# A selective scan on one core: units of 32 channels by 4 states in place of 8 channels by 16 states

## The chip, the core and the metric

The kernel runs on one core of a Trainium2 chip. A core has five engines that work from queues of their own, each in its own order: TensorE (PE), VectorE (DVE), ScalarE (ACT), GpSimd (POOL) and SyncE (SP), which here issues all the DMAs. The DMAs are carried by 16 DMA engines that the queue shares out. The metric is device time in microseconds (us) of one launch; lower is better.

## The reference, cut to what matters

The input is a batch of 8 images of 64 x 64 tokens with 192 channels. Two layers follow each other. Layer 0 is a state-space layer whose scan the kernel computes by matrix products over chunks, followed by a small MLP. Layer 1 splits the channels: one half goes through three convolutions, the other half through a depthwise convolution and a selective scan in four directions, a layer norm, a gate and a projection. The change touches only the selective scan of layer 1:

```python
D_HALF, D_INNER, D_STATE, DT_RANK, K = (96, 192, 16, 6, 4)
x_dbl = jnp.einsum('bkdl,kcd->bkcl', xs4, x_proj_w)
dts = x_dbl[:, :, :DT_RANK]
Bs = x_dbl[:, :, DT_RANK:DT_RANK + D_STATE]
Cs = x_dbl[:, :, DT_RANK + D_STATE:]
delta = jax.nn.softplus(jnp.einsum('bkrl,kdr->bkdl', dts, dt_proj_w) + dt_proj_b[None, :, :, None])
A = -jnp.exp(A_logs)

def step(h, t):
    u_t, d_t, b_t, c_t = t
    h = jnp.exp(d_t[..., None] * A) * h + (d_t * u_t)[..., None] * b_t[:, :, None, :]
    return (h, jnp.einsum('bkdn,bkn->bkd', h, c_t))
...
ys = jnp.moveaxis(ys, 0, -1) + Ds[None, :, :, None] * xs4
```

Each of 8 images has 4 directions, 192 channels and 16 states, so 8 x 4 x 192 x 16 = 98,304 sequences of 4,096 tokens. Each needs a decay exp(delta A), an input delta u B, the recurrence, a product with C and a sum over the 16 states. delta and u depend on the channel, B and C on the state; a unit of 128 partitions that holds channels and states together must have all four repeated to the shape of the unit.

## The kernel before

A unit of the scan is one tile of 128 partitions by 1,024 tokens (`LC`). Its partitions are 8 channels (`UD`) by 16 states: partition 8n + c is state n of channel c. There are 3,072 units: 8 images, 2 pairs of directions, 4 pieces of 1,024 tokens, 3 tiles of 128 channels (`t` = 0, 2, 1; two directions of a pair share the three tiles) and 16 units in each tile. `steps` are the pairs and pieces, `tiles` the tiles, and `units` numbers all units with q.

For each tile, `prepare` makes delta (softplus on ACT, L1406) and du = delta u on POOL (L1409), stores delta to DRAM (`dld`, L1412), splits du into three bf16 terms (two casts on ACT, L1417 and L1421, two subtractions on POOL, L1419 and L1423), stores those (`dud`, L1426) and loads them back in 12 DMAs as `dus` (L1434). For each step, `project` computes the rows of B, C and dt by matmul and stores B and C to DRAM (`bcd`), and `lay` (L1386) loads each back repeated to 128 partitions.

For each unit q the work is:

- `fetch` (L1445): one DMA of 512 KB brings 8 rows of delta, repeated 16 times, from DRAM into a `dA` tile. It is issued six units ahead (`AHEAD`), into seven buffers.
- `decay` (L1450): ACT turns that tile in place into exp(delta A), two units ahead.
- `spread` (L1458): PE spreads du over the states into PSUM `dB`, two matmuls, one unit ahead, in two buffers.
- `weigh` (L1473): DVE multiplies `dB` in PSUM with the repeated B.
- `scan` (L1480): DVE runs the recurrence; then POOL multiplies h with C in place, on all columns but the last (L1482).
- `carry_on` (L1488, L1489): ACT copies the last column to the carry of the next piece and then multiplies that column with C.
- `gather` (L1500): every four units PE sums over the states, in two halves of four matmuls side by side in 32-column groups; ACT copies each half out of PSUM (L1505), and four DMAs of 8 rows store it (`store`, L1513).

Layer 0 of the next image and the rest of layer 1 of other images run beside the scan. `Beside` holds them as generators; after each half unit `half` lets them issue instructions until a credit in estimated PE time is used up, so every engine's queue interleaves scan and side work in the order in which the Python code issues them (`pin` keeps that order). All DMAs stand in SP's queue in the same order. PSUM has eight banks: four rotate among all side work and the scan's small results (`cx.one`), four are the two buffers of `dB`.

The repeating DMAs have their source pattern from `repeated`:

```python
n = rows.shape[0]
row, col = [list(d) for d in rows.ap]
dims = [row, [0, 128 // n]] if inner else [[0, 128 // n], row]
return bass.AP(rows.tensor, rows.offset, dims + [col])
```

The outermost dimension of the source is thus the number of copies in `fetch` and the number of rows in `lay`; the destination is 128 partitions of 4 KB.

Of the kernel before, what the change touches and what calls it, by code (L numbers as in the profile page):

```python
# [39 lines left out]
UD = 128 // NS  # L40
UN = 128 // UD
# [68 lines left out]
def setup(cx, cp, dp, p0, p1):  # L110
# [141 lines left out]
    fold = cp.tile([128, UD], F32, tag="fold", name="fold")  # L252
    nc.vector.tensor_copy(fold, ident[:, 0:UD])
    for i in [32 * g + UD * v for g in range(4) for v in range(3)][1:]:
        nc.vector.tensor_add(fold, fold, ident[:, i : i + UD])
    for g in range(4):
        nc.vector.tensor_copy(
            k["spread"][32 * g : 32 * (g + 1), :].rearrange("p (n c) -> p n c", c=UD),
            bcast(fold[32 * g : 32 * (g + 1), 0:UD], 1, NS),
        )  # L260
    col = cp.tile([128, UD], F32, tag="col", name="col")
    nc.vector.tensor_copy(col, ident[:, 0:UD])
    for n in range(1, NS):
        nc.vector.tensor_add(col, col, ident[:, UD * n : UD * (n + 1)])
    k["gather"] = cp.tile([128, 32], F32, tag="gather", name="gather")
    nc.gpsimd.memset(k["gather"], 0.0)
    nc.vector.tensor_copy(k["gather"][:, 0:UD], col)
# [110 lines left out]
def conv0(cx, x):  # L378
# [3 lines left out]
    with cx.pool("cw0") as wp, cx.pool("v0", 2) as vp:  # L382
# [51 lines left out]
        def convolve(p, j):  # L434
            pss = [cx.one("ps_cv") for i in range(2)]
            yield from depthwise(cx, pss, [diag[0:64, j], diag[64:128, j]], pads[j])
            for i, ps in enumerate(pss):
                xc = xcs[p, 2 * j + i] = vp.tile([128, 512], F32, tag="xc", name="xc", bufs=7)
                pin(nc.scalar.activation(xc, ps, AF.Silu, bias=k["cb"][:, 2 * j + i : 2 * j + i + 1]))
# [73 lines left out]
def ssd(cx):  # L513
# [16 lines left out]
    with cx.pool("g0", 2) as gp, cx.pool("s0", 2) as sp:  # L530
# [126 lines left out]
        def outputs(c):  # L657
# [19 lines left out]
            yield None  # L677
            psh = [cx.one("ps_h")[:, :INNER0] for d in range(2)]
# [7 lines left out]
            ps = pss[1].rearrange("p (h c) -> p h c", c=HP)  # L686
            pin(nc.vector.tensor_add(Hn, ps, Hn))
# [31 lines left out]
def mlp0(cx, x, x1):  # L719
# [9 lines left out]
    with cx.pool("mw0") as wp, cx.pool("m0", 2) as mp:  # L729
# [8 lines left out]
        def loads(i):  # L738
# [10 lines left out]
            def load_y(v, d):  # L749
                t = mp.tile([128, 2, INNER0], F32, tag=f"y{d}", name=f"y{d}", bufs=4 - 2 * d)  # L750
# [561 lines left out]
def selective_scan(cx, us, ys, beside, images, start_image, tail):  # L1312
# [9 lines left out]
    AHEAD, BEHIND = 6, 2  # L1322
# [6 lines left out]

    units = [(n, i) for n in range(len(tiles)) for i in range(UN)]  # L1330
    U = len(units)
# [12 lines left out]
    with (  # L1344
# [4 lines left out]
        tc.tile_pool(name="ps1w", bufs=2, space=PSUM) as pw,  # L1349
    ):  # L1350
        u_of, rows_of, bc_of, delta_of, du_of, carries = {}, {}, {}, {}, {}, {}
        dAs, dBs, hs, late = {}, {}, {}, []
# [7 lines left out]
        def project(m):  # L1360
# [15 lines left out]
            yield  # L1376
            yield
            bcd = dp.tile([4 * NS, LC], F32, tag="bcd", name="bcd")
            pin(nc.sync.dma_start(out=bcd, in_=rows[0 : 4 * NS]))
            rows_of[m] = rows, bcd  # L1380

        def lay(m, e, i):

            t = wp.tile([128, LC], F32, tag=f"bc{i}{e}", name=f"bc{i}{e}")
            at = NS * (2 * i + e)
            pin(nc.sync.dma_start(out=t, in_=repeated(rows_of[m][1][at : at + NS], True)))  # L1386
            bc_of.setdefault((m, e), []).append(t)

        def prepare(n):
# [8 lines left out]
            dl, du = (wp.tile([128, LC], F32, tag=v, name=v) for v in ("dl", "du"))  # L1398
            pss = [cx.one("ps_dt") for here in halves]
            for ps, at, here in zip(pss, DTS, halves):  # L1400
                took = slice(at, at + 2 * RK)
                pin(nc.tensor.matmul(ps, lhsT=k["dtw"][took, g, t, :], rhs=rows[took, here], start=True, stop=True))
            beside.spend(1.2)
            yield 1
            for ps, here in zip(pss, halves):
                pin(nc.scalar.activation(dl[:, here], ps, AF.Softplus, bias=bias))  # L1406
            cx.exp_again()
            yield 3
            pin(nc.gpsimd.tensor_mul(du, dl, u_of[m][t]))  # L1409
            yield 6  # L1410
            dld = dp.tile([128, LC], F32, tag="dld", name="dld")
            pin(nc.sync.dma_start(out=dld, in_=dl))  # L1412
            delta_of[n] = dld
            yield 7

            terms = wp.tile([128, 3, LC], BF16, tag="terms", name="terms")
            pin(nc.scalar.copy(terms[:, 0, :], du))  # L1417
            yield 9
            pin(nc.gpsimd.tensor_sub(du, du, terms[:, 0, :]))  # L1419
            yield 11  # L1420
            pin(nc.scalar.copy(terms[:, 1, :], du))  # L1421
            yield 13
            pin(nc.gpsimd.tensor_sub(terms[:, 2, :], du, terms[:, 1, :]))  # L1423
            yield 17
            dud = dp.tile([3, 128, LC], BF16, tag="dud", name="dud")
            pin(nc.sync.dma_start(out=dud.rearrange("s p l -> p s l"), in_=terms))  # L1426
            yield 21

            dus = np_.tile([128, UN // 2, 512], BF16, tag="dus", name="dus")
            for half in range(2):  # L1430
                for odd in range(2):
                    at = 32 * (2 * odd + half)
                    for v in range(3):
                        pin(nc.sync.dma_start(  # L1434
                            out=dus[at + UD * v : at + UD * (v + 1)],
                            in_=dud[v].rearrange("(i odd c) l -> odd c i l", odd=2, c=UD)[odd][:, :, halves[half]],
                        ))
# [82 lines left out]
        for i in range(2):  # L1520
            lay(0, 0, i)
# [217 lines left out]
```

## Time and profile before

| what | value |
|---|---|
| median of 3 runs | 16,427.84 us (16,426.35 to 16,461.0) |
| profiled execution, first to last instruction | 16,436.7 us |
| PE busy | 13,372.1 us, 81% of the span |
| DVE busy | 12,230.0 us, 74% |
| POOL busy | 10,527.5 us, 64% |
| ACT busy | 10,412.7 us, 63% |
| DMA, main queue | 3,227.83 MB in 1,601,496 packets, 78.5% of 16 engines' span |
| mean granted TensorE clock | 0.827 of full speed |
| scan, 3,072 times on DVE (L1480) | 2,344 ns each, 7,200.8 us |
| product with B on DVE (L1473) | 1,216 ns each, 3,736.3 us |
| product with C on POOL (L1482) | 2,354 ns each, 7,228.8 us |
| decay on ACT (L1450) | 1,144 ns each, 3,512.9 us |
| sum over the states on PE (L1500) | 730 ns each, 4 side by side, 2,364.1 us |

The profile lists the span of the profiled execution and no other time of it; the span is 0.05% above the median of the runs. The busy times are unions over the span: a PE that is busy may be waiting in its pipeline. The first scan starts at 902 us and the last at 16,193 us, so the span has about 870 us in front of the scan stage and 240 us behind it. Between them a unit takes 5.0 us on average, of which DVE has 3.56 us for the two operations of the scan. In the tables of idle time, the engine or DMA named after an arrow is the one whose end released the waiting instruction.

### The profile page before, as it was taken

The page shows a single profiled execution, that of the slowest core. Times are in us where ns is not written, and L with a number is a line of the kernel's source. Part 1 is how long each engine was busy: PE and PEld are TensorE (multiplying, and loading weights), DVE is VectorE, ACT ScalarE, POOL GpSimd, SP SyncE. Part 2 cuts the span into 40 slices and gives each one's busy share as a digit, 9 for nine tenths or more (in the row PEclk, how much of TensorE's full clock was granted, in tenths as well). Part 3 has the DMA queues.
Part 4 walks back from the last instruction along what each step waited for, and adds up shares of the span by engine and source line. Part 5 has one row for each costly group of instructions (what it writes and reads, how often), then busy time and mean ns, then how long its engine had stood idle before and what let it go on. Part 6 is the DMA issues. An engine that isn't in the chain of part 4 may idle for free.

```text
span 16436.7 us, 210821 instructions
## 1 busy us (share of the span) xinstructions
PE 13372.1 (81%) x69608; PEld 4636.5 (28%) x69608; DVE 12230.0 (74%) x9264; ACT 10412.7 (63%) x20023; POOL 10527.5 (64%) x5766
## 2 busy tenths in 40 slices
PE   8977887788877897878888788777898788878876
PEld 4423322332223321333223332233322333211111
DVE  2178887886878767887678876788767886778994
ACT  4466677665775757757576575766657666655654
POOL 3158766775668656686567765677656775566773
PEclk9987888789887897878888798887988779877766
DMA  3288888788887888878888778887778877888885
GB/s 89 84 218 195 210 205 225 190 204 208 204 219 187 205 205 207 209 191 204 208 208 207 198 196 198 217 205 197 204 193 221 198 202 205 193 227 200 211 204 137
DMA packets 1602582, 3241.31 MB, mean 197 GB/s; under 512 B 390152, under 2 KB 841368, under 8 KB 1601496
## 3 DMA queue, kind: packets, MB, share of 16 engines
q1 hardware_dynamic: 1601496, 3227.83, 78.5%
q8 instruction: 559, 9.16, 0.3%
q14 instruction: 527, 4.32, 0.1%
HBM read 2548.91 MB, written 678.18 MB: 196 GB/s over the span
## 4 chain that ended last, share of the span: by engine, by line
PE 30%; DMA 16%; DVE 14%; ACT 13%; POOL 7%; issue 5%; SPq 2%; DVEq 0%; ACTq 0%; POOLq 0%
DVE h L1480 9%; DMA dA<-dld 5%; PE acc L1500 5%; DVE dB L1473 4%; PE ps_c L895 4%; PE ps_cv L343 3%; POOL h L1482 3%; ACT dA L1450 3%; PE dB L1458 2%; DMA dus<-dud 2%; PE ps_sum L1193 1%; ACT L107 1%; PE ps_m L799 1%; PE ps_y L696 1%; ACT h L830 1%
## 5 line engine op out<-in xcount | busy, mean ns | idle before, releaser
L1482 POOL TENSOR_TENSOR h<-h,bc 128x1023 f32<-128x1023 f32 x3072 | 7228.8, 2354 | 4585.2 <-DVE h L1480 3895.8
L1480 DVE TENSOR_TENSOR_SCAN h<-dA,carry,dB 128x1024 f32<-128x1024 f32 x3072 | 7200.8, 2344 | 820.7 <-ACT dA L1450 257.6
L1473 DVE TENSOR_TENSOR dB<-dB,bc 128x1024 f32<-128x1024 f32 x3072 | 3736.3, 1216 | 1827.5 <-PE dB L1458 1823.9
L1450 ACT ACTIVATE dA<-dA,neg_a 128x1024 f32<-128x1024 f32 x3072 | 3512.9, 1144 | 29.3 <-DMA dA<-dld 24.1
L1500 PE MATMUL acc<-h,gather 128*32 128x512 f32 x12288 | 2364.1, 730 | 596.5 <-ACT h L1489 329.0
L1458 PE MATMUL dB<-dus,spread 24*128 24x512 bf16 x6144 | 1370.2, 435 | 664.5 <-DVE h L1480 620.1
L1505 ACT COPY y<-acc 128x512 f32<-128x512 f32 x1536 | 884.8, 576 | 750.3 <-PE acc L1500 677.4
L895 PE MATMUL ps_c<-p,conv_w 96*96 96x512 f32 x2304 | 1287.7, 685 | 37.9 <-ACT p L915 26.9
L1488 ACT COPY carry<-h 128x1 f32<-128x1 f32 x3072 | 584.2, 190 | 856.9 <-DVE h L1480 854.4
L1458 PEld LDWEIGHTS <-spread 24*128 24x128 bf16 x6144 | 308.0, 93 | 2837.2 <-issue 1395.5
L1489 ACT ACTIVATE h<-h,bc 128x1 f32<-128x1 f32 x3072 | 905.2, 295 | 143.3 <-ACT carry L1488 1.8
L696 PE MATMUL ps_y<-X,M 64*64 64x64 f32 x12288 | 605.6, 270 | 418.6 <-issue 232.7
L624 ACT ACTIVATE M<-ps_d,ln_dt 128x64 f32<-128x64 f32 x3072 | 669.1, 335 | 314.6 <-PE ps_d L630 304.6
L343 PE MATMUL ps_cv<-pad,diag 64*64 64x512 f32 x6912 | 841.0, 605 | 7.1 <-ACT y L1505 5.1
L1500 PEld LDWEIGHTS acc<-h,gather 128*32 128x32 f32 x12288 | 311.2, 117 | 1636.3 <-issue 1040.1
L107 ACT ACT_TABLE_LOAD x577 | 740.3, 1283 | 10.0
L696 PEld LDWEIGHTS ps_y<-X,M 64*64 64x64 f32 x12288 | 548.8, 180 | 606.5 <-issue 275.5
L629 PE MATMUL ps_d<-R,after 128*128 128x384 f32 x1024 | 606.4, 685 | 31.2 <-ACT bc L618 14.6
L895 PEld LDWEIGHTS ps_c<-p,conv_w 96*96 96x96 f32 x2304 | 372.6, 180 | 785.5 <-issue 725.4
L618 ACT COPY bc<-ps_t 64x256 f32<-64x256 f32 x256 | 93.4, 365 | 716.7 <-PE ps_t L613 716.5
L373 PE MATMUL ps_h<-oa,w1a 128*128 128x256 f32 x1536 | 484.0, 438 | 76.6 <-ACT y L1505 32.2
L1370 PE MATMUL ps_xp<-u,xp 128*108 128x512 f32 x768 | 470.0, 699 | 92.5 <-DMA u<-u 76.0
(243 smaller groups left out, 18412.4 us busy)
## 6 DMA issues: line engine op xcount, KB each, us to landing
dA<-dld SPq DMA_DIRECT2D x3072, 512.0 KB
dud<-terms SPq DMA_DIRECT2D x192, 768.0 KB
dus<-dud SPq DMA_DIRECT2D x2304, 64.0 KB
bc<-bcd SPq DMA_DIRECT2D x256, 512.0 KB
y<-yrows SPq DMA_DIRECT2D x256, 384.0 KB
u<-u SPq DMA_DIRECT2D x192, 512.0 KB
dld<-dl SPq DMA_DIRECT2D x192, 512.0 KB
y<-y SPq DMA_DIRECT2D x3072, 32.0 KB
```

The lines of the kernel that those rows point to most:

```text
L107: self.pin(self.nc.scalar.preload_act_table_set("natural_log_exp_and_others"))
L343: pin(nc.tensor.matmul(ps[64 * b : 64 * (b + 1)].rearrange("p (h w) -> p h w", w=WW), lhsT=diag[:, t, :], rhs=pad[64 * i : 64 * (i + 1), b ...
L696: pin(nc.tensor.matmul(psy[d][here, h * HP : (h + 1) * HP], lhsT=M[here, d, h, :], rhs=X[here, d, h, :], start=True, stop=True,))
L895: pin(nc.tensor.matmul(ps.rearrange("p (h w) -> p h w", w=WW), lhsT=w[:, t, :], rhs=pad[:, dy : dy + RB, dx : dx + WW], start=t == 0, stop ...
L1450: pin(nc.scalar.activation(dAs[q], dAs[q], AF.Exp, scale=k["neg_a"][:, steps[m][1], t, i : i + 1]))
L1458: pin(nc.tensor.matmul(dBs[q][:, half, :], lhsT=k["spread"][at : at + 3 * UD, :], rhs=du_of[n][at : at + 3 * UD, i // 2, :], start=True, s ...
L1473: pin(nc.vector.tensor_mul(dBs[q], dBs[q], of(q)[0]))
L1480: pin(nc.vector.tensor_tensor_scan(order(h, g), order(dA, g), order(dB, g), carry, ALU.mult, ALU.add))
L1482: pin(nc.gpsimd.tensor_mul(h[:, rest], h[:, rest], C_[:, rest]))
L1489: pin(nc.scalar.activation(end, end, AF.Identity, scale=C_[:, last : last + 1]))
L1500: pin(nc.tensor.matmul(ps[32 * v : 32 * (v + 1)], lhsT=k["gather"], rhs=hs[q - 3 + v][:, here], start=True, stop=True))
L1505: pin(nc.scalar.copy(y[:, here], ps))
```

## The change

A unit becomes 32 channels by 4 states (partition 32n + c). A tile of 128 channels still has 16 units: 4 groups of channels, each with 4 units of 4 states. The order in a tile is by pairs of groups: 8 units (`GROUP`) take the four states of two groups in turn.

- delta and du are both fetched repeated: one DMA of 512 KB each for a group of 32 channels, used by its four units, in three buffers each (`dlr`, `dur`). The fetches for the next 8 units are issued at the odd units of the present 8: delta and du of the first group at units 1 and 3, of the second at units 5 and 7.
- B takes the place that du had: it is split into three bf16 terms on 32 rows in `project`, stored, loaded by `lay_b` in four small DMAs, and spread over the channels by `spread`. The terms of du and their casts, subtractions and DMAs are gone; du is made in place of u.
- C is laid by `lay_c`: four DMAs of 512 KB for each direction in place of one (4 rows, each repeated 32 times).
- The product with C goes to a new tile `g` (four buffers) and covers all columns; the second ACT operation of `carry_on` is gone, its copy is left out for the last piece, and it runs two units behind instead of one.
- `gather` runs every two units and adds the four states up in one PSUM tile of its own; one copy and two DMAs of 64 rows store a pair of groups.
- The rotating PSUM buffers go from four to three, `xc` from 7 to 6 buffers, `y0` and `y1` of the MLP from 4 and 2 to 3 and 2, `h` from 7 to 3, and one addition in `ssd` moves in front of two matmuls.

```diff
-UD = 128 // NS
-UN = 128 // UD
+UD = 32
+NU = 128 // UD
+UN = 128 // UD * (NS // NU)
...
-    AHEAD, BEHIND = 6, 2
+    BEHIND, GROUP = 2, 8
...
+        def of(q):
+
+            n, i = divmod(q, UN)
+            pair, i = divmod(i, GROUP)
+            state, b = divmod(i, 2)
+            return n, *tiles[n], 2 * pair + b, state
...
+        def lay_c(m, e, state):
+
+            t = wp.tile([128, LC], F32, tag=f"c{e}{state}", name=f"c{e}{state}")
+            at = NS * e + NU * state
+            pin(nc.sync.dma_start(out=t, in_=repeated(rows_of[m][2][at : at + NU], True)))
...
-        def fetch(q):
-            n, i = units[q]
-            dAs[q] = np_.tile([128, LC], F32, tag="dA", name="dA", bufs=AHEAD + 1)
-            pin(nc.sync.dma_start(out=dAs[q], in_=repeated(delta_of[n][UD * i : UD * (i + 1)], False)))
+        def fetch(q, which):
+
+            n, _, _, cg, _ = of(q)
+            tag = ("dl", "du")[which]
+            t = np_.tile([128, LC], F32, tag=tag + "r", name=tag + "r", bufs=3)
+            pin(nc.sync.dma_start(out=t, in_=repeated(delta_of[n][which][UD * cg : UD * (cg + 1)], False)))
+            reps[n, cg, which] = t
...
-            pin(nc.vector.tensor_mul(dBs[q], dBs[q], of(q)[0]))
+            pin(nc.vector.tensor_mul(dBs[q], dBs[q], reps[n, cg, 1]))
...
-            h = hs[q] = np_.tile([128, LC], F32, tag="h", name="h", bufs=4 + BEHIND + 1)
+            h = hs[q] = np_.tile([128, LC], F32, tag="h", name="h", bufs=3)
             pin(nc.vector.tensor_tensor_scan(order(h, g), order(dA, g), order(dB, g), carry, ALU.mult, ALU.add))
-            rest = slice(1, LC) if last == 0 else slice(0, LC - 1)
-            pin(nc.gpsimd.tensor_mul(h[:, rest], h[:, rest], C_[:, rest]))
+            gs[q] = np_.tile([128, LC], F32, tag="g", name="g", bufs=4)
+            pin(nc.gpsimd.tensor_mul(gs[q], h, bc(q)[1][of(q)[-1]]))
...
+            for half in range(2):
+                for b in range(2):
+                    at = 64 * half + UD * b
                     pin(nc.tensor.matmul(
-                        ps[32 * v : 32 * (v + 1)], lhsT=k["gather"], rhs=hs[q - 3 + v][:, here], start=True, stop=True
+                        ps[at : at + UD], lhsT=k["gather"], rhs=gs[q - 1 + b][:, halves[half]],
+                        start=state == 0, stop=state == NS // NU - 1,
                     ))
...
-                if q + AHEAD < U:
-                    fetch(q + AHEAD)
+                ahead = q - q % GROUP + GROUP
+                if q % 2 == 1 and ahead < U:
+                    i = q % GROUP // 2
+                    fetch(ahead + i // 2, i % 2)
...
-    cx.singles = [ctx.enter_context(tc.tile_pool(name="ps", bufs=4, space=PSUM))]
+    cx.singles = [ctx.enter_context(tc.tile_pool(name="ps", bufs=3, space=PSUM))]
```

## The prediction, made before the changed kernel ran

> **What bounds the kernel now.** I read the page first: engine shares, DMA, then the chain that ended last.
>
> ```profile
> PE 13372.1 (81%) x69608; PEld 4636.5 (28%) x69608; DVE 12230.0 (74%) x9264; ACT 10412.7 (63%) x20023; POOL 10527.5 (64%) x5766
> ...
> q1 hardware_dynamic: 1601496, 3227.83, 78.5%
> ...
> PE 30%; DMA 16%; DVE 14%; ACT 13%; POOL 7%; issue 5%; SPq 2%; DVEq 0%; ACTq 0%; POOLq 0%
> DVE h L1480 9%; DMA dA<-dld 5%; PE acc L1500 5%; DVE dB L1473 4%; PE ps_c L895 4%; PE ps_cv L343 3%; POOL h L1482 3%; ACT dA L1450 3%; PE dB L1458 2%; DMA dus<-dud 2%; PE ps_sum L1193 1%; ACT L107 1%; PE ps_m L799 1%; PE ps_y L696 1%; ACT h L830 1%
> ```
>
> Nothing is full on the average, and the chain passes from engine to engine: a coupled pipeline with DMA in it. The groups give the price of each step of a unit, the list of DMAs their sizes, and the waits show who holds whom:
>
> ```profile
> L1489 ACT ACTIVATE h<-h,bc 128x1 f32<-128x1 f32 x3072 | 905.2, 295 | 143.3 <-ACT carry L1488 1.8
> L1505 ACT COPY y<-acc 128x512 f32<-128x512 f32 x1536 | 884.8, 576 | 750.3 <-PE acc L1500 677.4
> ...
> dA<-dld SPq DMA_DIRECT2D x3072, 512.0 KB
> ...
> bc<-bcd SPq DMA_DIRECT2D x256, 512.0 KB
> ...
> y<-y SPq DMA_DIRECT2D x3072, 32.0 KB
> ```
>
> ```profile
> DVE dB L1473 <- PE dB L1458: 1823.9, 718, 99.4
> ...
> PE acc L1500 <- ACT h L1489: 329.0, 96, 15.9
> ...
> SPq L1445 <- DVE h L1480: 3764.0, 1460, 11.0
> ```
>
> Last, busy time in stretches (columns: stretch, length, then busy us of PE, PEld, DVE, ACT, POOL; clock; DMA share; GB/s):
>
> ```profile
> 836.00:840.00 4.00, 0.00 (x0) 0.00 (x0) 0.00 (x0) 0.00 (x0) 0.00 (x0) 0.50 1.07 374
> 898.00:912.00 14.00, 2.17 (x7) 0.31 (x6) 9.72 (x6) 10.02 (x14) 6.38 (x3) 0.50 1.04 232
> ...
> 4500.00:4600.00 100.00, 48.93 (x150) 11.52 (x148) 54.28 (x33) 52.57 (x79) 46.12 (x23) 0.64 0.90 227
> 5000.00:5400.00 400.00, 310.94 (x2551) 135.49 (x2549) 335.87 (x345) 230.07 (x624) 330.55 (x218) 0.76 0.77 191
> 5900.00:6200.00 300.00, 269.10 (x723) 72.28 (x722) 182.08 (x107) 141.69 (x259) 164.52 (x87) 0.90 0.84 211
> ```
>
> The first two decide my forecast. At 836 us plain 4 KB rows move at 374 GB/s over 16 engines that are all busy: 23.4 GB/s an engine, 175 ns a packet. At 898 us, where the repeating fetches fill the queue, 16 busy engines move only 232 GB/s: 14.5 GB/s, 282 ns a packet. In the record of all packets, 4 KB ones average 259 ns (shortest 159). At 4,500 us, between images, DMA is full while every engine is half idle.
>
> **A count of DMA engines.** A DMA's semaphore gets one event from each DMA engine that carried a part. The 14,153 DMAs left 188,810 events. That comes out if every DMA with 16 or more rows outermost counts 16, and each of the 5,376 with 8 rows on both sides (`dus`, and the y stores of L1513) counts 9: eight engines, and one event by the issuer. The outermost dimension sets the number of engines. The old `fetch` has 16 copies outermost, the old `lay` 16 rows: 16 engines. The new `fetch` has 4 copies outermost, the new `lay_c` 4 rows. No DMA of before has 4 against 128 partitions, so the ends are 16 engines and 4; the nearest rows, those of 8, speak for 4, and I take that.
>
> **The change part by part.** I sum against the profiled span, 16,436.7 us; the median of the runs is 16,427.84, 0.05% below.
>
> *ACT.* Gone: casts of du, 192 x (1,035 + 1,046) ns = 400 us; L1489, 905; 1,152 of 1,536 copies of L1505, 664; a quarter of the 3,072 carry copies at 190, 146. Added: 256 copies of 32x512 for B, at most the 576 of L1505 each, 147. Net -1,970 us: 10,413 becomes 8,445. PE's 329 us of waiting for L1489 goes; next latest for `gather` is POOL's product (PE waits 64 us for it now), asked for every two units instead of four.
>
> *POOL.* Gone: 384 subtractions, 817 us. Added: 256 at 32x512, at most the 1,265 ns of a 128x512 row, 324. The product covers 1,024 columns instead of 1,023. Net -490.
>
> *PE, DVE.* `spread` and `gather` issue as many matmuls of the same size as before, the two operations of the scan are the same: 0. The addition in `ssd` moved ahead, three rotating PSUM buffers and fewer `xc` and y buffers: the 1,536 results of L1500 leave the rotation, so I take 0, between -329 and +400 (twice the wait for L1489 as a bound); the DMA below covers it, and without that cover it is the third rival.
>
> *SP.* 14,153 DMAs become 8,905 (fetches 3,072 to 1,536, 2,304 of `dus` to 512 of `lay_b`, y stores 3,072 to 768, `lay_c` 512 for 256). Issuing gets cheaper; the 3,764 us in which SP waited for a scan to free a `dA` buffer go. In their place the fetch of the second group's delta waits for the decay of unit 6, that of its du for the product of unit 6. Behind them in SP's queue stand all side loads and stores. The du is needed three units later: three scans and two products, 3 x 2.34 + 2 x 1.22 = 9.5 us. Issue to landing of a fetch took 7.7 us in the middle and 17.0 at the 95th percentile of the record.
>
> *DMA bytes.* Fetches 1,611 to 805 MB, `dus` and `dud` 302 to 101, C and B rows 151 to 302, y stores the same 101. In all 3,228 to 2,372 MB, -27%.
>
> *DMA on the four engines.* 1,536 fetches and 512 `lay_c` are 2,048 DMAs of 128 packets of 4 KB; on four engines that is 32 packets each, 65,536 packets an engine. At 175 ns: 11.5 ms; at 282: 18.5. For 282 speaks that it is the same kind of transfer. Against it: I suppose that engines slow each other only while they write neighbouring partitions at once, and 32 packets a DMA let them drift apart more than 8 did; fewer engines may also meet less traffic. I take the middle, 228 ns: 15.0 ms.
> The rest on such an engine (1 KB packets average 98 ns, 2 KB ones 108): of 12.9 ms now (78.5% of the span) I take off fetch and `lay` (3,328 x 8 x 259 ns = 6.9), half of `dus` and y stores, which use half the engines ((2,304 x 8 x 98 ns + 3,072 x 259 ns) / 2 = 1.3), `dud` (192 x 24 x 108 ns = 0.5), and add du's store, the new y stores and B's rows (about 0.7). That is 4.9 ms, 0.3 of it outside the scan stage: 4.6.
> Scan stage 15.0 + 4.6 = 19.6 ms, plus 0.87 before it and 0.24 behind: 20.7 ms. Per unit 6.4 us against 5.0 now; PE, DVE, ACT and POOL (4.4, 4.0, 2.7 and 3.3 us a unit at most) fit beneath. Ends: 17.2 ms at 175 ns, 24.2 ms at 282.
>
> **The Trainium skill beside these rows.** In "DMA: Bandwidth & Descriptors", section "Rules for kernel authors", it says that a leading zero-stride broadcast of c copies confines the whole DMA to at most c engines, and in "Why a DMA increments its semaphore by 16 and not by 1" that the number of engines must divide the slowest dimension on both sides. That agrees with the 9 events of the 8-row DMAs, and speaks against this change: by it 20.7 ms, without it the 15.2 of the first rival. In "SBUF — State Buffer", section "Door 1", partitions p and p+32 share one port of 27 GB/s. Four engines that each write 32 partitions would pair up on ports; an estimate from that page is 301 ns a packet and 25.5 ms; the row of 282 ns at 898 us is nearer the truth here.
>
> **The rivals.**
> 1. *All 16 engines carry the new fetches: faster.* Against it the 9 events. Then the DMA time falls from 12.9 to 4.9 + 2,048 x 8 x 259 ns = 9.1 ms, -29%. Of the chain's shares, DMA (16%, 2,630 us) gives 760, ACT (13%, busy -19%) 400, POOL 55: 15.2 ms, from 14.6 to 16.2.
> 2. *Four engines, but at the plain 175 ns.* They are busy 16.1 of a scan stage of 15.3 ms; with the others' work partly beside: 16.5 to 18.0, say 17.2 ms.
> 3. *16 engines, but the look-ahead is too short.* The second group's fetches land later than 9.5 us after issue, and DVE stands still once in eight units. It eats rival 1's 1.2 ms from 3.2 us per eight units on (384 of them): a quarter of the fetches now land after 11.1 us. About 16.8 ms.
>
> **How the numbers follow.** Forecast (four engines, 190 to 282 ns: 18.0 to 24.2) 0.66; rival 1 0.13; rival 2 0.16; rival 3 0.05. The predicted time is the forecast's 20.7 ms. From 16.5 to 24.2 ms leaves out rival 1 and little else; the forecast's own range is 18.0 to 24.2. Runs differ by 0.2%, the least that can be told from no change. Faster: rival 1 and a bit of 2, 0.14; within 0.2%: 0.01; slower: 0.85.
>
> **What would show it.** Right: bytes near 2,370 MB, yet four engines full for (15.0 + 4.9) / 20.7 = 96% and twelve for 24%, a mean DMA share near 42%; about 118,000 landing events, as 2,048 DMAs count 5 (141,000 if they count 16); DVE waits in the thousands of us for `dur`, ACT for `dlr`; all engines less busy by share. ACT's busy time near 8.4 ms and POOL's near 10.0 show those steps. Wrong: `dur` and `dlr` hardly in the waits, a DMA share that follows the bytes, and a unit below 5 us, which is rival 1. If the waits for `dur` are there with 16 events for each fetch, it is rival 3.

## The result, and the profile after

The changed kernel takes 19,097.96 us (median of four runs, 19,068.96 to 19,171.84) against 16,427.1 us before: 1.163 times as long, 95% interval 1.160 to 1.166. The profiled execution took 19,085.77 us, its span 19,083.8 us.

First the page of the changed kernel: busy times, the main DMA queue (packets, MB, share of the time of 16 engines), and the start of the chain that ended last.

```profile
PE 14168.6 (74%) x69608; PEld 4792.8 (25%) x69608; DVE 12223.5 (64%) x9251; ACT 8669.1 (45%) x14912; POOL 10030.2 (53%) x5637
...
q1 hardware_dynamic: 1220568, 2371.92, 40.8%
...
DMA 7%; DVE 5%; PE 4%; ACT 2%; issue 1%; POOL 1%; SPq 0%; DVEq 0%; POOLq 0%; ACTq 0%
```

Bytes, ACT and POOL fell as their parts of the change say, every engine is less busy by share, and the time rose by 2,670 us. The chain is followed back over only a fifth of the span this time, so its shares say who is on it and no prices; DMA leads it. The groups and the waits of the changed kernel (group: busy, mean ns | idle before, releaser; wait: us in total, times, longest) show where the engines stand:

```profile
L1489 DVE TENSOR_TENSOR dB<-dB,dur 128x1024 f32<-128x1024 f32 x3072 | 3740.3, 1218 | 4203.4 <-DMA dur<-dud 2594.1
L1460 ACT ACTIVATE dA<-dlr,neg_a 128x1024 f32<-128x1024 f32 x3072 | 3510.5, 1152 | 2862.3 <-DVE h L1496 1829.1
```

```profile
DVE dB L1489 <- DMA dur<-dud: 2594.1, 241, 131.0
DVE dB L1489 <- PE dB L1474: 1515.7, 609, 17.5
...
ACT dA L1460 <- DMA dlr<-dld: 1007.5, 161, 33.8
...
POOL g L1498 <- DVE h L1496: 6665.7, 2101, 46.6
```

The instructions cost what they did; the new idle time stands before `weigh`, and the fetch of du ends it. 241 waits of 10.8 us on the average: DVE stands still for as long as its own work on three units takes, and POOL stands behind it.

The record of DMA packets shows why a queue that is busy 40.8% on the average can be late. The 8,905 DMAs left 118,410 landing events (one event for each DMA engine that carried a part, and one of the issuer where these are fewer than 16). To within six events that is what results if each of the 1,536 fetches and 512 `lay_c` counts 5 (four engines and the issuer), each of the 512 loads of B's terms, which have 12 rows, counts 13, and every other DMA 16. The prediction's count of the kernel before has the same six too many. In the main queue exactly four packets are in flight during 46% of the span, at least four during 84%, and none during 12%; before, none were during 12% as well, but exactly four during 0.7% only. From issue to landing a fetch takes 8.1 us at best, 13 to 14 us in the middle and 33 to 35 us at the 95th percentile; before it was 4.2, 7.7 and 17.0 us.

### The profile page after: what moved, and what is told of

The parts are those of the page before. It is cut to its first block, busy times and chain, and to the rows that moved or that the text cites. A ratio compares the mean times of both kernels' runs of the same rounds, so it can differ in the third digit from the quotient of the medians.

```text
span 19083.8 us, 196810 instructions
## 1 busy us (share of the span) xinstructions
PE 14168.6 (74%) x69608; PEld 4792.8 (25%) x69608; DVE 12223.5 (64%) x9251; ACT 8669.1 (45%) x14912; POOL 10030.2 (53%) x5637
## 3 DMA queue, kind: packets, MB, share of 16 engines
q1 hardware_dynamic: 1220568, 2371.92, 40.8%
## 5 line engine op out<-in xcount | busy, mean ns | idle before, releaser
L1498 POOL TENSOR_TENSOR g<-h,c 128x1024 f32<-128x1024 f32 x3072 | 7227.9, 2353 | 7499.4 <-DVE h L1496 6665.7
L1489 DVE TENSOR_TENSOR dB<-dB,dur 128x1024 f32<-128x1024 f32 x3072 | 3740.3, 1218 | 4203.4 <-DMA dur<-dud 2594.1
L1460 ACT ACTIVATE dA<-dlr,neg_a 128x1024 f32<-128x1024 f32 x3072 | 3510.5, 1152 | 2862.3 <-DVE h L1496 1829.1
L1474 PE MATMUL dB<-b,spread 12*128 12x512 bf16 x6144 | 1362.8, 441 | 1742.9 <-DVE h L1496 1727.1
L1518 PE MATMUL acc<-g,gather 128*32 128x512 f32 x12288 | 2488.4, 760 | 143.1 <-POOL g L1498 88.0
L1474 PEld LDWEIGHTS <-spread 12*128 12x128 bf16 x6144 | 298.0, 93 | 3988.3 <-DVE h L1496 2283.4
L1518 PEld LDWEIGHTS acc<-g,gather 128*32 128x32 f32 x12288 | 317.7, 119 | 1541.8 <-issue 912.7
L1433 PE MATMUL ps_dt<-rows,dtw 12*128 12x512 f32 x768 | 465.8, 804 | 231.6 <-ACT dl L1430 180.3
L597 POOL TENSOR_TENSOR R<-upto,da 128x768 f32<-128x768 f32 x256 | 376.3, 1470 | 189.2 <-PE ps_d L627 178.0
L1440 POOL TENSOR_TENSOR u<-dl,u 128x1024 f32<-128x1024 f32 x192 | 452.1, 2355 | 10.8 <-ACT dl L1437 10.8
```

Of the source, the lines that this page charges most:

```text
L1460: pin(nc.scalar.activation(dAs[q], reps[n, cg, 0], AF.Exp, scale=k["neg_a"][:, steps[m][1], t, i : i + 1]))
L1474: pin(nc.tensor.matmul(dBs[q][:, half, :], lhsT=k["spread"][at : at + 3 * NU, :], rhs=b[at : at + 3 * NU, state // 2, :], start=True, stop ...
L1489: pin(nc.vector.tensor_mul(dBs[q], dBs[q], reps[n, cg, 1]))
L1498: pin(nc.gpsimd.tensor_mul(gs[q], h, bc(q)[1][of(q)[-1]]))
L1518: pin(nc.tensor.matmul(ps[at : at + UD], lhsT=k["gather"], rhs=gs[q - 1 + b][:, halves[half]], start=state == 0, stop=state == NS // NU - 1,))
```

## The experiments

**1. The same unit with the channels outermost.** Only the order of the partitions changes: partition 4c + n in place of 32n + c. Then delta and du have 32 rows outermost in the source, each repeated 4 times, and C has 32 copies outermost. The matrices of `spread` and `gather` and the decay's scales follow the new order; work, buffers, sizes and the order of instructions are those of the changed kernel.

```diff
-            k["spread"][32 * g : 32 * (g + 1), :].rearrange("p (n c) -> p n c", c=UD),
-            bcast(fold[32 * g : 32 * (g + 1), :], 2, UD),
+            k["spread"][32 * g : 32 * (g + 1), :].rearrange("p (c n) -> p c n", n=NU),
+            bcast(fold[32 * g : 32 * (g + 1), :], 1, UD),
...
-            pin(nc.sync.dma_start(out=t, in_=repeated(rows_of[m][2][at : at + NU], True)))
+            pin(nc.sync.dma_start(out=t, in_=repeated(rows_of[m][2][at : at + NU], False)))
...
-            pin(nc.sync.dma_start(out=t, in_=repeated(delta_of[n][which][UD * cg : UD * (cg + 1)], False)))
+            pin(nc.sync.dma_start(out=t, in_=repeated(delta_of[n][which][UD * cg : UD * (cg + 1)], True)))
...
```

> The partitions of a unit stand as 4c + n instead of 32n + c, with the spread and gather matrices and the decay's scales in that order. The repeating sources of fetch and of lay_c then have 32 outermost (32 rows each 4 times, 32 copies of 4 rows) instead of 4; bytes, number of DMAs and all engine work stay. Forecast's theory (the four DMA engines that carry fetch and lay_c are the bound): 16 engines each, about 141,000 landing events instead of 118,410, waits for dur and dlr together under 500 us instead of 3,602, and the time that the first rival worked out, 15.2 ms (14.6 to 16.2). Theory 'the rest costs' (three PSUM buffers, gather every two units, h in three buffers): 18 ms or more. Theory 'look-ahead' (a fetch is asked for too late whatever carries it): 16.5 to 18, with waits for dur still over 1,000 us.

Measured: 16,558.36 us, ratio to before 1.0086 (1.0069 to 1.0103). 2,540 us are back with nothing but the outermost dimension. There are 140,938 landing events, 22,528 more, which is 2,048 DMAs at 16 in place of 5; a fetch lands after 3.3 us at best and 4.8 to 5.4 us in the middle. No packet is in flight during 45% of the span. The page and the waits of this kernel:

```profile
PE 13814.6 (83%) x69608; PEld 4745.1 (29%) x69608; DVE 12213.0 (74%) x9251; ACT 8662.1 (52%) x14912; POOL 10032.3 (61%) x5637
...
q1 hardware_dynamic: 1245144, 2372.02, 45.2%
```

```profile
DVE dB L1489 <- PE dB L1474: 1543.0, 683, 12.7
DVE Hm L669 <- PE ps_s L663: 499.5, 216, 7.1
DVE Hn L677 <- POOL Hn L671: 342.5, 151, 7.8
...
DVE dB L1489 <- DMA dur<-dud: 147.5, 17, 106.5
```

The mean DMA share is higher than with four engines (45.2 against 40.8%) in a shorter time, and the wait for du is gone (the longest, 106.5 us, is the start). The events and the waits came out as the forecast's theory says, and neither of the others fits: the time is far below 18 ms, and the wait for du far below 1,000 us. That settles the loss: four engines. The time did not come down to the expected 14.6 to 16.2 ms, which leaves a second question: 16 engines, 27% fewer bytes and 1.75 ms less on ACT, and yet not faster than before.

**2. Only the fetches, or only C, over 16 engines.** In the first kernel each fetch is four DMAs of 32 rows; in the second each `lay_c` is four DMAs of one row repeated 32 times. By landing events each of these counts 16.

```diff
-            pin(nc.sync.dma_start(out=t, in_=repeated(delta_of[n][which][UD * cg : UD * (cg + 1)], False)))
+            for v in range(NU):
+                pin(nc.sync.dma_start(out=t[UD * v : UD * (v + 1)], in_=delta_of[n][which][UD * cg : UD * (cg + 1)]))
```

> The layout of the changed kernel; each fetch as four DMAs of 32 rows to 32 partitions (outermost dimension 32 on both sides), lay_c as in the changed kernel, on four engines. 4,608 more DMAs to issue. Forecast's theory: an engine of the four now has 1,536 x 8 + 512 x 32 = 28,672 packets of 4 KB instead of 65,536, so it is no longer full: 15.2 to 16.4 ms, C's DMAs the late ones. 'The rest costs': 18 ms or more. 'Look-ahead': 16.5 to 18.

```diff
-            pin(nc.sync.dma_start(out=t, in_=repeated(rows_of[m][2][at : at + NU], True)))
+            for v in range(NU):
+                row = rows_of[m][2][at + v : at + v + 1]
+                pin(nc.sync.dma_start(
+                    out=t[UD * v : UD * (v + 1)], in_=bass.AP(row.tensor, row.offset, [[0, UD], [1, LC]])
+                ))
```

> The layout of the changed kernel; each lay_c as four DMAs of one row repeated over 32 partitions (16 engines), fetches as in the changed kernel, on four engines. Forecast's theory: 53,248 packets of 4 KB on each of the four instead of 65,536, so about 12,300 x 172 ns = 2.1 ms less work on them: 17.0 to 18.2 ms. 'Look-ahead' and 'the rest costs': 18.8 or more, since C is asked for long before it is used.

Measured: 17,599.67 us (ratio 1.0728, 1.0703 to 1.0753) with the fetches spread, 18,496.1 us (1.1265, 1.1247 to 1.1284) with C spread. So C alone on four engines costs 17,600 - 16,558 = 1,040 us, and the fetches alone 1,940; both together 2,540, less than the sum. The waits for du, of the kernel with spread fetches:

```profile
DVE dB L1490 <- DMA dur<-dud: 1103.6, 124, 121.0
```

Both forecasts were too fast. With spread fetches a `lay_c` takes 15.0 us in the middle, and a part of du that is ordered while one is under way lands after 14.6 us in the middle, against 3.3 us otherwise (6.4 and 4.6 us for the fetches of experiment 1). I read it so that a fetch over 16 engines also has a part on the four that carry C, and lands when its last part does.

**3. du asked for earlier, still on four engines.** The fetches are ordered at units 1, 2, 3 and 5 of eight in place of 1, 3, 5 and 7, with four `dur` and three `g` buffers.

```diff
-                if q % 2 == 1 and ahead < U:
-                    i = q % GROUP // 2
-                    fetch(ahead + i // 2, i % 2)
+                when = {1: (0, 0), 2: (0, 1), 3: (1, 1), 5: (1, 0)}
+                if q % GROUP in when and ahead < U:
+                    b, which = when[q % GROUP]
+                    fetch(ahead + b, which)
```

> The changed kernel with four buffers for the repeated du (g in three instead of four to make room) and du of the two groups fetched at units 2 and 3 of the eight instead of 3 and 7, without a wait on a product; the number of engines stays 4. Forecast's theory: the four engines are busy about 85% of the 19.1 ms, so it can't go under 16.3 ms; the wait for dur falls by half or more, part of it comes back as waits for dlr: 17.8 to 18.8. 'Look-ahead': 16.4 ms or less. 'The rest costs': 18.8 to 19.2.

Measured: 18,480.06 us, ratio 1.1262 (1.124 to 1.1285): 620 us better than the changed kernel. The waits of this kernel:

```profile
DVE dB L1489 <- PE dB L1474: 2102.6, 768, 24.5
ACT dA L1460 <- DMA dlr<-dld: 1755.8, 219, 34.2
...
DVE dB L1489 <- DMA dur<-dud: 188.1, 28, 131.7
```

The wait for du became one for delta (1,008 to 1,756 us) and one for PE: earlier orders move the queue on the four engines about, they don't empty it. So 620 us of the 2,540 hang on the order of the fetches, with the buffers that go with it; with the better order, four engines still cost 1,920.

**4. Where the gain stayed: a table by stretch of an image.** From the ends of the scans in the record I took us per unit in blocks of 48 units (mean of images 2 to 7). With the channels outermost, the last three blocks are 5.17, 5.20 and 4.28 us against 5.74, 5.26 and 4.64 before: there the change gains. Blocks 2 and 3, beside which `ssd` (the state-space layer of the next image) runs, are 6.35 and 6.22 against 5.69 and 5.68: most of what is lost. Block 5 loses too (5.31 against 5.05), and no run here looks into it. One image's two blocks in the table by stretches, before and with the channels outermost (stretch, length, busy us of PE, PEld, DVE, ACT, POOL; clock, DMA share, GB/s):

```profile
6857.00:7406.00 549.00, 409.45 (x3272) 175.37 (x3270) 453.58 (x450) 320.33 (x832) 440.00 (x287) 0.74 0.76 188
```

```profile
7000.00:7603.00 603.00, 447.55 (x3314) 190.87 (x3312) 450.50 (x449) 265.00 (x697) 425.05 (x282) 0.70 0.43 130
```

The same 96 units and the same side work take 54 us longer though DMA and ACT have less to do. Two edits touch this place: the addition to `Hn` that moved, and the fourth rotating PSUM bank that went. The first was put alone into the kernel before:

```diff
+            ps = pss[1].rearrange("p (h c) -> p h c", c=HP)
+            pin(nc.vector.tensor_add(Hn, ps, Hn))
             psh = [cx.one("ps_h")[:, :INNER0] for d in range(2)]
...
-            ps = pss[1].rearrange("p (h c) -> p h c", c=HP)
-            pin(nc.vector.tensor_add(Hn, ps, Hn))
```

> The kernel before with one line moved as in the change: in ssd the addition to Hn stands before the two matmuls of ps_h. Counted in scan units, the kernel with the channels outermost loses its time in the 96 units of an image that run beside ssd (6.35 and 6.22 us a unit there, 5.69 and 5.68 before), some 58 us an image, 460 us in all. Theory A (the order costs it, because DVE and PE now wait for POOL's product Hn): 16,870 us. Theory B (the missing fourth rotating PSUM bank costs it): 16,430 us here. Theory C (something of the scan units themselves costs it): 16,430 us here too.

Measured: 16,713.44 us, ratio 1.0172 (1.0152 to 1.0192): 288 us from one line, theory A's sign and 63% of the 460 us. Blocks 2 and 3 take 6.08 us a unit in place of 5.69 and 5.68, the others are unchanged. The wait in front of the moved addition, before and with the line moved:

```profile
DVE Hn L687 <- POOL Hn L673: 229.5, 153, 8.1
```

```profile
DVE Hn L679 <- POOL Hn L673: 573.1, 221, 8.1
```

The two matmuls of `ps_h` stood between POOL's product and the addition that needs it; without them DVE, which has the next scan queued behind, waits 344 us more for POOL's product.

**5. The price of less DMA and ACT by itself.** The kernel before, with each fetch bringing half of the columns, decay reading that half twice, and L1489 left out (so delta is wrong in half of the columns, and the last column isn't weighted with C).

```diff
-            pin(nc.sync.dma_start(out=dAs[q], in_=repeated(delta_of[n][UD * i : UD * (i + 1)], False)))
+            pin(nc.sync.dma_start(
+                out=dAs[q][:, halves[1]], in_=repeated(delta_of[n][UD * i : UD * (i + 1), halves[1]], False)
+            ))
...
-            pin(nc.scalar.activation(end, end, AF.Identity, scale=C_[:, last : last + 1]))
```

> The kernel before with less work in DMA and ACT: each fetch brings half of the columns (256 KB, 805 MB less in all, as much as the change takes off its fetches), decay reads that half twice, and L1489 is left out, so delta is wrong in half of the columns and the last column is not weighted with C. It does alone what the first rival of the prediction counted as gain. If the shares of the chain are prices: DMA -760 us (2 KB packets at 108 in place of 259 ns take 3.7 of 12.9 ms off), ACT 8.7% less busy of 2,137 us on the chain, -190: 15.5 ms. If DMA and ACT lie beside the others: 16.3 to 16.43 ms. From the units of the kernel with the channels outermost that do not run beside ssd (34 us an image less): 16.15 ms.

Measured: 15,830.9 us, ratio 0.9639 (0.9624 to 0.9653). The page of this kernel:

```profile
PE 13118.1 (83%) x69608; PEld 4578.7 (29%) x69608; DVE 12212.4 (77%) x9264; ACT 9561.3 (60%) x16951; POOL 10529.5 (67%) x5766
...
q1 hardware_dynamic: 1601496, 2422.52, 57.0%
```

594 us, between the two readings: there was a gain in DMA and ACT, 63% of what the shares of the chain gave for this kernel (950 us). So the change with 16 engines, whose savings are of about this size (856 MB and 1,750 us of ACT against 805 MB and 851 us here), had about that much to win, and lost more than it elsewhere.

**6. Freeing the bank of `ps_s` early.** The kernel of experiment 1; ACT copies the second `ps_s` to SBUF as soon as it is there, and POOL adds it.

```diff
+            s1 = sp.tile([2 * N0, NH, HP], F32, tag="s1", name="s1", bufs=1)
+            pin(nc.scalar.copy(s1.rearrange("p h c -> p (h c)"), pss[1]))
             ps = pss[0].rearrange("p (h c) -> p h c", c=HP)
             pin(nc.vector.tensor_add(Hm, ps, Hm))
...
+            pin(nc.gpsimd.tensor_add(Hn, Hn, s1))
...
-            ps = pss[1].rearrange("p (h c) -> p h c", c=HP)
-            pin(nc.vector.tensor_add(Hn, ps, Hn))
```

> The changed kernel with the channels outermost in the unit, and in ssd ACT copies the second result ps_s to SBUF as soon as it is there, so that its bank comes free without POOL's product, and POOL adds it to Hn in place of DVE. Theories A and B (ssd waits for POOL's product with its banks held): 16,100 to 16,400 us against 16,560 without the copy, and faster than before if all 460 us come back. Theory C: 16,560 us, less at most the 140 us that DVE saves on 256 additions.

Measured: 16,293.23 us, ratio 0.9919 (0.9904 to 0.9934): 265 us less than in experiment 1, and 0.8% less than before. The edit frees the bank and also takes away DVE's wait for POOL's product (342.5 us in experiment 1); the run doesn't tell the two apart. Blocks 2 and 3 fall to 5.97 and 5.76 us, not to 5.69 and 5.68 or below, so something else stays. The waits that are left:

```profile
DVE dB L1490 <- PE dB L1475: 1551.5, 687, 12.7
DVE Hm L671 <- PE ps_s L663: 568.7, 220, 7.3
...
PE acc L1519 <- ACT y L1530: 48.8, 20, 4.8
```

**7. Two more buffers that were under suspicion.** Du earlier as in experiment 3, and, apart from it, four `dA` buffers, both on the kernel of experiment 6.

```diff
-            dAs[q] = np_.tile([128, LC], F32, tag="dA", name="dA", bufs=3)
+            dAs[q] = np_.tile([128, LC], F32, tag="dA", name="dA", bufs=4)
...
-            gs[q] = np_.tile([128, LC], F32, tag="g", name="g", bufs=4)
+            gs[q] = np_.tile([128, LC], F32, tag="g", name="g", bufs=3)
```

> The changed kernel with channels outermost and ACT's copy of ps_s (16,293 us), and du asked for two to five units earlier (orders at units 1, 2, 3 and 5 of eight; four dur buffers, three g buffers). If the look-ahead still holds it (DVE waits 137 us for du): 16,130 to 16,220 us. If those waits lie in a time that another wait would fill, or the third g buffer holds POOL back: 16,270 to 16,400 us.

> The same kernel (16,293 us) with four dA buffers in place of three, and three g buffers in place of four: ACT waits 1,157 us for a scan to free a dA buffer, with its copies and softplus queued behind. If that queue is what holds PE and DVE: 15,900 to 16,150 us, and ACT's waits for the scan below 500 us. If ACT's waiting is idle time that costs nothing: 16,270 to 16,350 us.

Measured: 16,290.23 us (0.9913, 0.9889 to 0.9937) and 16,271.72 us (0.9907, 0.9878 to 0.9937): neither can be told from experiment 6. With 16 engines the look-ahead is long enough. ACT's wait for a `dA` buffer, in experiment 6 and with four buffers, was idle time that cost nothing:

```profile
ACT dA L1461 <- DVE h L1497: 1157.5, 594, 7.3
```

```profile
ACT dA L1461 <- DVE h L1497: 244.1, 89, 5.9
```

**8. The change's banks in the kernel before.** The kernel before with the change's banks: one for `acc`, three that rotate, and what that needs.

```diff
-                ps = cx.one("acc")
+                ps = py.tile([128, 512], F32, tag="acc", name="acc")
...
-    cx.singles = [ctx.enter_context(tc.tile_pool(name="ps", bufs=4, space=PSUM))]
+    cx.singles = [ctx.enter_context(tc.tile_pool(name="ps", bufs=3, space=PSUM))]
```

> The kernel before with the PSUM banks of the change: one bank for acc alone, three that rotate, the moved line in ssd and the two dt matmuls one after the other; units, fetches and the four-unit sums as before. The moved line alone gave 16,713 us. Theory B2 (the fourth rotating bank has a price of its own, beside ssd and mlp0): 16,900 to 17,300 us, with longer waits of ACT for ps_t and ps_z. Theory D (the banks cost nothing, and what the changed kernel with channels outermost still lacks against the kernel with the half fetches, some 460 us, is in its fetches and buffers): 16,650 to 16,750 us.

Measured: 17,955.04 us, ratio 1.0936 (1.09 to 1.0972), 1,240 us above the moved line alone. But the waits of this kernel show a new one that the changed kernel has not:

```profile
PE acc L1505 <- ACT y L1510: 935.8, 490, 15.3
```

The old sum needs two banks in quick succession, and here the second half waits until ACT has emptied the only one. The time lies above both theories, and this run doesn't tell the price of the rotating bank. Nor can it be had by taking one of the four banks away and leaving the sums in the rotation: in that version of the kernel before the waits close a circle (a deadlock), and it has no time.

**9. Four rotating banks in the changed kernel.** The kernel of experiment 6, but each gather writes into a rotating bank, four banks rotate, and only the last of four gathers is copied out: three of the four parts of the sum over the states are left out, the work on every engine stays.

```diff
-            if state == 0:
-                late.append(py.tile([128, 512], F32, tag="acc", name="acc"))
-            ps = late[-1]
+            ps = cx.one("acc")
...
-                        start=state == 0, stop=state == NS // NU - 1,
+                        start=True, stop=True,
...
-    cx.singles = [ctx.enter_context(tc.tile_pool(name="ps", bufs=3, space=PSUM))]
+    cx.singles = [ctx.enter_context(tc.tile_pool(name="ps", bufs=4, space=PSUM))]
```

> The kernel with channels outermost and ACT's copy of ps_s (16,293 us), but the sum over the states does not add up in a bank of its own: each of the four gathers writes into a rotating bank, and only the last one is copied out, so y holds one of four parts; work on every engine stays the same, and four banks rotate again. Theory B2 (the missing fourth bank holds the side work): 15,800 to 16,050 us, nearest the 15,831 us of the kernel with half the fetches, with shorter waits of ACT for ps_t, ps_z and ps_d. Theory D (the banks cost nothing once the copy is in; what is missing lies in the units and fetches): 16,250 to 16,350 us. Slower than 16,400 us would say that the gathers hold the rotation up.

Measured: 15,564.15 us, ratio 0.9465 (0.9449 to 0.9481): 729 us for four rotating banks in place of three and one for `acc`, more than theory B2 expected. The bank of `acc` by itself had held PE for 48.8 us in experiment 6, so I take nearly all of it for the fourth bank of the rotation. The page and waits of this kernel:

```profile
PE 13160.0 (84%) x69608; PEld 4502.8 (29%) x69608; DVE 12073.9 (77%) x8995; ACT 8740.9 (56%) x15168; POOL 10270.5 (66%) x5893
```

```profile
DVE dB L1489 <- PE dB L1474: 1049.6, 514, 7.9
DVE h L1496 <- ACT carry L1506: 354.4, 204, 5.1
DVE Hm L671 <- PE ps_s L663: 327.0, 186, 7.3
```

Against experiment 6, 500 us have gone from DVE's wait for `spread` and 240 from that for `ps_s`. PE works off its queue in order, so that a side matmul that waits for a bank holds up the `spread` behind it; I read the 500 us that way, which no run shows by itself. Beside `ssd` a unit takes 5.31 and 5.36 us, less than before the change.

**10. The whole sum with four rotating banks.** The four units of one group of 32 channels follow each other; their products are kept in seven `g` buffers, and 16 matmuls of 256 columns, four quarters side by side, add the states up at once in a rotating bank. Room for the products comes from C: five buffers in place of eight, each loaded about four units before its use. Fetches are ordered two groups ahead. ACT's copy of `ps_s` stays.

```diff
-    BEHIND, GROUP = 2, 8
+    BEHIND, GROUP = 2, 4
...
+            ps = cx.one("acc")[:, : LC // 4]
+            for v in range(GROUP):
+                for w in range(4):
+                    pin(nc.tensor.matmul(
+                        ps[UD * w : UD * (w + 1)], lhsT=k["gather"], rhs=gs[q - 3 + v][:, LC // 4 * w : LC // 4 * (w + 1)],
+                        start=v == 0, stop=v == GROUP - 1,
+                    ))
...
-            t = wp.tile([128, LC], F32, tag=f"c{e}{state}", name=f"c{e}{state}")
+            t = wp.tile([128, LC], F32, tag="c", name=f"c{e}{state}", bufs=5)
```

> The kernel of 16,293 us (channels outermost, ACT's copy of ps_s) with four rotating PSUM banks again and the whole sum: the four units of one group of 32 channels follow each other, their four products are kept (seven g buffers), and 16 matmuls of 256 columns, four quarters side by side, add the states up at once in a rotating bank that ACT empties right after. Room for the products comes from C: five buffers in place of eight, each loaded about four units before its use. Fetches are asked for two groups ahead. Theory B2 (the fourth bank was what held the side work): 15,450 to 15,800 us, as the 15,564 us of the kernel that leaves three of four parts of the sum out. Rival: C arrives late, or SP stands behind the buffers of C (four products to be waited for in 24 units): 15,900 to 16,300 us, with waits of POOL for c.

Measured: 15,692.69 us, ratio 0.9534 (0.9507 to 0.956), the best kernel here that leaves nothing out: 4.7% less time than before, 17.8% less than the changed kernel. It is in the range of theory B2, and 600 us below experiment 6 with the whole sum; the order of the units, the fetches and the buffers of C differ from experiment 6 as well. The page of this kernel, and its two blocks beside `ssd`:

```profile
PE 12948.9 (82%) x81896; PEld 5029.6 (32%) x81896; DVE 12082.2 (77%) x8995; ACT 8763.0 (56%) x15534; POOL 10274.5 (65%) x5893
...
q1 hardware_dynamic: 1331160, 2372.17, 47.4%
```

```profile
6642.00:7149.00 507.00, 397.20 (x3641) 183.56 (x3640) 434.97 (x414) 278.57 (x744) 455.16 (x315) 0.76 0.50 153
```

507 us for the stretch that took 549 before and 603 in experiment 1. POOL waits 13 us in all for C; SP waits 1,440 us for POOL's products to free buffers of C, and the time bears it.

## Why the prediction was right, and where not

The sign, the mechanism and the range held; the 20.7 ms were 1.6 ms too much, and they came that near because two errors partly cancelled, which was luck: a packet was cheaper than supposed, and the engines that carried it weren't full.

*Four engines from the outermost dimension: right.* The forecast of about 118,000 landing events came out as 118,410, and the layout with 16 engines alone took 2,540 of the 2,670 us away. The Trainium skill's rule that a zero-stride leading dimension of c copies confines a DMA to at most c engines ("DMA: Bandwidth & Descriptors", section "Rules for kernel authors") agrees with both counts, 5 events with 4 copies outermost and 16 with 32.

*The price of a packet, 228 ns: the term that was mis-sized.* While four or five packets are in flight, the record has 173 ns for one of 4 KB. Taken from the load: at least four are in flight during 84% of the span, nearly the time the four engines work; less the 4.9 ms of other traffic that the prediction puts on each of them, 11 to 12 ms are left for 65,536 packets, 170 to 180 ns (an estimate). That is 3 to 4 ms below the 15.0. The 282 ns of the stretch at 898 us belonged to 16 engines all busy. The supposition behind the middle value, that engines slow each other only while they write neighbouring partitions, wasn't tested by itself. (By the same sum 190 ns gives 18.2 ms and 301 ns 25.4 ms, not 18.0 and 25.5; nothing hangs on it.)

*Engines full for 96%: wrong the other way.* With 173 ns in place of 228 the prediction's own sum gives 11.3 + 4.6 + 0.87 + 0.24, about 17.0 ms. The 2 ms from there to the measured time are time in which these engines aren't full: at least four packets are in flight during 84% of the span, 16.0 ms. One reason, as I read it, is that the orders don't come evenly. The four of C fall among the fetches of a few units, and du that is ordered while a `lay_c` is under way lands after 21.8 us in the middle, 11.6 us otherwise; experiment 3 got 620 us back from another order. How the 2 ms divide between this and the price of the banks below wasn't measured. A price near the second rival's, on engines that aren't full, thus gives 19.1 ms: above the second rival's 18.0 and inside the forecast's own range, though for a mixture of the two.

*The estimate from ports* that the prediction cites from the Trainium skill ("SBUF — State Buffer", section "Door 1"), 301 ns a packet, isn't seen: four engines that each write 32 partitions move 4 KB in 173 ns. The estimate supposed that two engines write p and p+32 at the same moment all the time, and no run shows that they do.

*ACT 8,445 us, POOL 10.0 ms, 2,372 MB:* measured 8,669 us, 10,030 us and 2,371.92 MB. ACT's 224 us lie mostly in L1489, which was counted with its whole 905 us: busy times are unions, 189 of these us overlapped other work of ACT, and 717 went. The waits of DVE in the thousands for du (2,594 us) and of ACT for delta (1,008) are there.

*PSUM and the moved line at 0, between -329 and +400: wrong, and hidden.* The moved line alone costs 288 us in the kernel before, and the fourth rotating bank 729 us on 16 engines, together more than the bound of +400 us (which isn't twice the wait of 329 us either). The argument that the sums leave the rotation, so that three banks do, counted users of banks and not how long each is held: by the code, `ssd` holds a bank of `ps_s` until POOL's product is done. Under the four engines this cost could be overlooked; how much of it shows in the 19.1 ms wasn't measured.

*The first rival, 15.2 ms, from the shares of the chain:* its layout gave 16.56 ms, and with the bank back and ACT's copy, 15.56 and 15.69 ms, inside its 14.6 to 16.2 (the first of the two leaves parts of the sum out). It saw neither the four engines nor the banks. DMA and ACT were worth 63% of their shares in experiment 5. *The third rival* (look-ahead too short on 16 engines) is refuted by the 147 us of waits and by experiment 7.

What stays open: how the 2 ms named above divide, the loss in block 5, what in experiment 6 is the bank and what DVE's wait, and the 130 us between experiments 9 and 10.

## What to carry to other kernels

When a load repeats rows, look at the outermost dimension of its pattern first: with 4 there, four DMA engines did the work of 16, and the mean DMA share (40.8%) looked relaxed while the engines waited; packets in flight and landing events tell it. Where one part of a change takes a PSUM bank or moves an instruction across engines to make room, price that part alone: here one bank and one line cost more than the saved 27% of the bytes and 1,750 us of ACT brought. And before believing that a stretch is bound by an engine, cut the image into stages and compare us per unit stage by stage; the loss and the gain sat in different ones.

## What the runs showed of the hardware

The time that PE counts as busy moves with its clock. Thirteen of the kernels here, before and after among them, issue the same 69,608 matmuls; their PE busy time goes from 13,118 us (15.8 ms, granted clock 0.841) to 14,276 us (17.9 ms, clock 0.789), and busy time times clock stays within 11,030 to 11,320 us (before: 13,372 x 0.827 = 11,060; after: 14,169 x 0.779 = 11,040). The changed kernel's 797 us of additional PE time thus go with the clock and not with more work (the ends of matmuls are modelled in the profile, so this is a reading of its busy time). It agrees in direction with the Trainium skill ("TensorE: Matmul & The Clock Gate", section "What's actually happening"): activity releases the throttle. By that a PE that is kept waiting would also be slower; how much of any loss here comes from it was not separated.

The price of a 4 KB packet isn't a constant of the pattern: 173 ns with four or five in flight in the changed kernel, 218 ns with 16 to 19, and 259 ns on the average in the kernel before, where 16 to 19 were in flight during 56% of the span. Nor is it a matter of their number alone: with 16 to 19 in flight it is 183 ns in experiment 1, where the same loads have the channels outermost, and 255 ns in the kernel before. Why wasn't tested.
